# A per-sample matrix product with residual: the channel exchange in three copies for five, the slots of x at multiples of 2048 bytes, two slots a turn in VectorE's loop

## The chip, the cores and the metric

The kernel runs on one core of a Trainium2 chip. The core has five engines that run side by side and meet at semaphores: TensorE (PE, matrix products into PSUM), VectorE (DVE), ScalarE (ACT), GpSimd (POOL) and SyncE (SP, used here to issue transfers). 16 DMA engines move data between HBM (the chip's main memory) and the SBUF, the on-chip memory of 128 partitions. SP and ACT each have a queue of transfers. The metric is the device time of one execution in microseconds (us), the median of several.

## What is computed

```python
x: (128, 128, 1024) float32            # batch, channel, time
itok_B_0_7: (128,) int32, 0 to 7       # which matrix a sample uses
L0_cond_weights: (8, 128, 128) float32

w = weights[subjects]
out = jnp.einsum('bct,bcd->bdt', x, w)
return x + out
```

Each of the 128 samples is a 128 x 1024 block of x (512 KB). It is multiplied by one of eight matrices and added to itself. 67.1 MB are read for x and 67.1 MB written.

## The kernel before

**Slots.** The SBUF holds `x_all`, 12 slots of 4 samples (`H * G = 2 * 2`), 16 KB in each partition and 2 MB in all. 32 slots' worth of work (`NT = 32`, 4 samples each) run through the 12 slots in turn. x_all starts at a multiple of `ALIGN` = 4096 bytes: 16,512 bytes of each partition are taken ahead of it, a filler `room` of 3,968 bytes follows, and x_all begins at byte 20,480. Behind it lie the weights `w_all`, the unit matrix `eye`, `aside` (4 KB in all 128 partitions), and four 128 x 128 weight tiles `ws`.

**Loads.** ACT issues two loads of 1 MB for a slot (`load`, issued at line 72), one for each half h. A load reads two samples as one stretch of HBM and writes 8 KB into each partition. With that, a partition has two neighbouring channels of one sample (partitions 0 to 63 the half's first sample, 64 to 127 its second), where the product wants one channel of each sample.

**Exchange.** `trade` (line 157 for all its copies, in the helper `move`) mends that on ACT. Seen as halves h and places s, `both[A:, 0]` (partitions 64 to 127, place 0) and `both[:A, 1]` (partitions 0 to 63, place 1) change places, with A = 64. Five copies do so: two of 64x1024 put `both[A:, 0]` aside (one half into partitions 0 to 63 of `aside`, the other into 64 to 127), one of 64x2x1024 moves `both[:A, 1]` to `both[A:, 0]`, and two of 64x1024 bring what was put aside to `both[:A, 1]`. Each copy raises `s_moved`; ACT waits on it between the three steps and at the end. The last wait raises `s_half[0]`, on which PE's product waits.

**ACT's loop** takes four slots a turn (`AHEAD = 4`): wait for the slot's load, issue the loads of the slot four ahead (if that place is empty, `s_empty`), then exchange.

**PE** (`multiply`, line 208) computes for each half two samples, four matmuls into PSUM. The weight tile it uses is the matrix plus `eye` (so the product already holds the residual), with rows in the order of the exchanged channels; VectorE makes it (`place`, line 197).

**VectorE's loop** takes four slots a turn (`TURN = 4`). For each half of a slot: wait for the product (`s_product`), copy 128x2048 from PSUM over the slot (line 223), make the next slot's two weight tiles for this half. `s_product` counts within a turn and is lowered in the turn's last half (line 220).

**Stores.** SP waits for both halves of a slot (`s_added`) and issues its store of 2 MB; for the last 12 slots it stores two slots at once (4 MB). Slot 0's store is written differently (line 319) and is cut into 4 KB packets. In the last three stores two slots are read as one run of 32 KB in each partition, in the others each slot is a run of 16 KB. In HBM each sample's channel is a row of 4 KB. The order of the work is set by these queues and semaphores alone; there is no planner.

Of the kernel before, what the change touches and what calls it, by code (L numbers as in the profile page):

```python
# [30 lines left out]
G = 2  # L31
H = 2
# [18 lines left out]
R = 2  # L51

AHEAD = 4

MOVES = 5

TURN = 4

PLACED = 16

ALIGN = 4096
QUEUES = {mybir.EngineType.SP: "qSPDynamicHW", mybir.EngineType.Activation: "qActDynamicHW"}


# [21 lines left out]
def kernel(  # L86
# [7 lines left out]
    nc = tc.nc  # L94
    B, C, T = x.shape
    S, _, D = weights.shape
    NT = B // (G * H)

    def sbuf(name, *shape, dtype=F32):
        return ctx.enter_context(nc.sbuf_tensor(name, list(shape), dtype)).ap()  # L100


    room = -(nc.sbuf_base + -nc.sbuf_base % 32) % ALIGN
    if room:
        sbuf("room", C, room // 4)
# [4 lines left out]
    ]  # L110
    w_all = sbuf("w_all", C, S, D)
    w_raw, w_mid, w_late = (xs[SLOTS - 1][:, q, :] for q in range(3))
    A = C // R
    eye = sbuf("eye", C, 1, D)
    mark = sbuf("mark", 1, 1)
    aside = sbuf("aside", C, T)
    spare = [aside[h * A : (h + 1) * A] for h in range(H)]
    ws = [sbuf(f"w{i}", C, 1, D) for i in range(H * G)]
    zeros = xs[SLOTS - 1][:, H * G - 1, :N]
    given, near, wrap = (  # L120
        xs[SLOTS - 1][:1, H * G - 1, N + k * B : N + (k + 1) * B].bitcast(I32) for k in range(3)
# [18 lines left out]
    s_moved = tc.alloc_semaphore("s_moved")  # L140
# [15 lines left out]
    def move(out, in_):  # L156
        nc.scalar.copy(out, in_).then_inc(s_moved, 1)  # L157
# [4 lines left out]
    def trade(k, slot):  # L162
        base = slot * (H * G * T)
        both = x_all[:, bass.ds(base, H * G * T)].rearrange("c (h s t) -> c s h t", h=H, s=G)
        for h in range(H):
            move(spare[h], both[A:, 0, h])
        nc.scalar.wait_ge(s_moved, k * MOVES + H)
        move(both[A:, 0], both[:A, 1])
        nc.scalar.wait_ge(s_moved, k * MOVES + H + 1)
        for h in range(H):  # L170
            move(both[:A, 1, h], spare[h])
        nc.scalar.wait_ge(s_moved, (k + 1) * MOVES).then_inc(s_half[0], 1)

    def store(i, n):
# [10 lines left out]
    def subjects_of(i):  # L185
        _, subject = nc.values_load_multi_w_load_instructions(
            index[0:1, i] if isinstance(i, slice) else index[0:1, bass.ds(i * (H * G), H * G)],
            engines=[mybir.EngineType.DVE],
            min_val=0,
            max_val=S - 1,  # L190
            skip_runtime_bounds_check_because="the index is clamped on the chip above",
        )
        return subject

    def place(h, subject):
        for q in range(h * G, (h + 1) * G):
            copy = nc.vector.tensor_tensor(  # L197
                ws[q], w_all[:, bass.ds(subject[q], 1), :], eye, ALU.add
            )
        copy.then_inc(s_half[h], 1 if h else PLACED)  # L200
# [16 lines left out]
    def copy(slot, n, h):  # L217
        mine = x_all[:, bass.ds(slot * (H * G * T) + h * G * T, G * T)]
        n = n * H + h + 1
        product = nc.vector.wait_ge(s_product, n)  # L220
        if n == TURN * H:
            product.then_inc(s_product, -n)
        nc.vector.tensor_copy(mine, ps[h].rearrange("d g t -> d (g t)")).then_inc(s_added, 1)  # L223

    with tc.tile_critical():  # L225
# [31 lines left out]
        for r in range(R):  # L257
            if r:
# [6 lines left out]
                1.0,  # L265
                base=r - r * R * A,
                channel_multiplier=R,
# [7 lines left out]
        with nc.scalar.Fori(0, NT // AHEAD) as turn:  # L275
            for k in range(AHEAD):
                landed(k)
                with nc.scalar.If(turn < NT // AHEAD - 1):
                    empty = nc.scalar.wait_ge(s_empty, k + 1)
                    if k + 1 == AHEAD:  # L280
                        empty.then_inc(s_empty, -AHEAD)
                    load(
                        k,
                        (turn * AHEAD + (k + AHEAD)) % SLOTS,
                        nc.s_assert_within(
                            turn * (AHEAD * H * G) + (k + AHEAD) * H * G,
                            0,
                            B - H * G,
                            skip_runtime_bounds_check_because="the last turn loads nothing",
                        ),  # L290
                    )
                trade(k, (turn * AHEAD + k) % SLOTS)
            nc.scalar.wait_ge(s_moved, AHEAD * MOVES).then_inc(s_moved, -AHEAD * MOVES)

# [35 lines left out]
        for h in range(H):  # L330
            place(h, subject)
        with nc.vector.Fori(0, NT // TURN) as turn:  # L332
            for n in range(TURN):
                subject = subjects_of(turn * TURN + (n + 1))
                for h in range(H):
                    copy((turn * TURN + n) % SLOTS, n, h)
                    place(h, subject)
# [42 lines left out]
```

## Time and profile before

| What | Value |
|---|---|
| Three runs | 323.84 us median (323.23 to 324.43) |
| The profiled execution | 323.75 us |
| Its span, first to last instruction | 321.9 us |
| Granted clock of TensorE, mean | 0.921 |
| Bytes over the span | HBM read 67.63 MB, written 67.11 MB: 419 GB/s |
| VectorE: copies from PSUM, line 223 | 64 of 128x2048, 2.292 us each |
| TensorE: matmuls, line 208 | 512 of 128x512, 0.624 us each |

In a profile, a group of instructions is shown by line, engine, operation and operands (out<-in), with how many there were, their busy time, the mean duration in ns, and the idle time of the engine just before them with what ended it. "issue" means that the profile shows nothing that the engine waited for. The DMA row gives the busy share of the 16 DMA engines in 40 equal slices of the span, in tenths (9 is 90% or more). A packet is the piece of a transfer that one DMA engine moves at a stretch; a queue's row gives its packets, the MB and the share of the 16 engines' time that the packets took. In the table of stretches each row has the length, the busy time of PE, PE's weight loads, VectorE, ACT and POOL (with the count of instructions), the granted clock of TensorE, the DMA share and GB/s.

### The profile page before, as it was taken

To read this page: it belongs to the slowest core of one execution; us is meant where nothing else is said; L and a number is where in the kernel's file an instruction comes from. 1 tells how busy PE (TensorE), PEld (TensorE's weight loads), DVE (VectorE), ACT (ScalarE), POOL (GpSimd) and SP (SyncE) were. 2 spreads that over 40 slices of the span, in tenths; PEclk is the share of its full clock that TensorE was granted. 3 is DMA by queue.
4 is the path that set the end of the run, shared out by engine and by line. 5 is a ranking of instruction groups with operands and counts; after the bars stand their busy time and mean duration, and the time that the engine had idled before them with its cause. 6 is when DMAs were issued, how large, how long until landed. Compare 5 with 4: busy or idle time off the path is not lost. (4 is left out here: it accounts for less than half of the span.)

```text
span 321.9 us, 2680 instructions
## 1 busy us (share of the span) xinstructions
PE 247.3 (77%) x528; PEld 102.7 (32%) x528; DVE 181.4 (56%) x217; ACT 195.7 (61%) x162; POOL 2.5 (1%) x10
## 2 busy tenths in 40 slices
PE   7279988888888888759949799496784989999000
PEld 3034333333333333324314343242332434443000
DVE  4708765666666666663634847266552676787300
ACT  1577767776777776677275772747727689990000
POOL 0200000000000000000000000000000000000000
PEclk9969999999999999998978979799996999999755
DMA  8999999999999999999999999999999999999995
GB/s 326 391 456 444 405 390 430 438 430 432 417 421 432 425 428 428 432 452 407 425 423 425 423 423 419 421 428 438 446 423 405 432 450 403 428 446 432 419 432 220
DMA packets 7732, 134.76 MB, mean 419 GB/s; under 512 B 1457, under 2 KB 1458, under 8 KB 2098
## 3 DMA queue, kind: packets, MB, share of 16 engines
q1 hardware_dynamic: 4658, 67.64, 49.8%
q10 hardware_dynamic: 3072, 67.11, 49.0%
q14 instruction: 2, 0.02, 0.0%
HBM read 67.63 MB, written 67.11 MB: 419 GB/s over the span
## 5 line engine op out<-in xcount | busy, mean ns | idle before, releaser
L208 PE MATMUL ps<-x_all,w 128*128 x512 | 238.8, 624 | 49.0 <-PEq L204 48.8
L223 DVE COPY x_all<-ps 128x2048 f32 x64 | 146.7, 2292 | 113.7 <-PE ps L208 107.4
L208 PEld LDWEIGHTS ps<-x_all,w 128*128 128x128 f32 x512 | 99.1, 199 | 188.6 <-issue 188.3
L157 ACT COPY aside<-x_all 64x1024 f32 x64 | 66.7, 1042 | 82.4 <-issue 79.1
L157 ACT COPY x_all<-aside 64x1024 f32 x64 | 66.8, 1044 | 1.8
L157 ACT COPY x_all<-x_all x32 | 60.7, 1897 | 3.9
L197 DVE TENSOR_TENSOR w<-w_all,eye 128x128 f32<-128x128 f32 x132 | 31.8, 283 | 0.8 <-issue 0.8
L235 PE MATMUL ps<-x_all 128*128 128x512 f32 x16 | 8.6, 697 | 1.7 <-DVE x_all L232 1.7
L235 PEld LDWEIGHTS ps<-x_all 128*128 128x128 f32 x16 | 3.6, 230 | 5.8 <-issue 4.2
L273 ACT ACT_TABLE_LOAD x1 | 1.3, 1283 | 6.2 <-issue 6.2
L299 DVE COPY w_all<-x_all 32x256 f32<-32x256 f32 x12 | 3.9, 326 | 0.4
L244 DVE STREAM_TRANSPOSE x_all<-x_all 128x512 f32<-128x512 f32 x2 | 2.0, 1076 | 3.1 <-DMA x_all<-in_L_cond_weights_dram 3.1
L299 POOL COPY w_all<-x_all 32x256 f32<-32x256 f32 x4 | 1.7, 425 | 6.6 <-DVE x_all L296 6.4
L296 DVE STREAM_TRANSPOSE x_all<-x_all 128x1024 f32<-128x1024 f32 x1 | 1.2, 1226 | 0.0
L232 DVE MEMSET x_all<- 128x512 f32 x1 | 0.5, 485 | 1.0 <-SPq L225 1.0
L250 DVE TENSOR_SCALAR x_all<-x_all 1x128 int32<-1x128 int32 x1 | 0.2, 215 | 0.3 <-DMA x_all<-in_itok_B_dram 0.3
L260 POOL TENSOR_SCALAR_AFFINE_SELECT eye<-x_all 128x128 f32<-128x128 f32 x1 | 0.3, 292 | 1.4 <-DVE x_all L232 1.4
L254 DVE CUSTOM_DVE_ANT_0 index<-x_all 1x256 uint16<-1x256 uint16 x1 | 0.3, 278 | 0.0
L260 POOL TENSOR_SCALAR_AFFINE_SELECT eye<-eye 128x128 f32<-128x128 f32 x1 | 0.3, 292 | 0.1
L252 DVE TENSOR_SCALAR x_all<-x_all 1x128 int32<-1x128 int32 x1 | 0.2, 215 | 0.0
L273 ACT COPY mark<-eye 1x1 f32<-1x1 f32 x1 | 0.2, 190 | 0.0
L367 POOL MEMSET const-bfloat16-1.0<- 128x1 bf16 x1 | 0.1, 101 | 0.0
(5 smaller groups left out, 0.4 us busy)
## 6 DMA issues: line engine op xcount, KB each, us to landing
x_all<-in_x_dram ACTq DMA_DIRECT2D x64, 1024.0 KB, 11.7
out_dram<-x_all SPq DMA_DIRECT2D x20, 2048.0 KB, 54.1
out_dram<-x_all SPq DMA_DIRECT2D x6, 4096.0 KB, 31.4
x_all<-in_L_cond_weights_dram SPq DMA_DIRECT2D x1, 512.0 KB, 3.8
x_all<-in_itok_B_dram SPq DMA_DIRECT2D x1, 0.5 KB
```

What stands on the lines that cost most here:

```text
L157: nc.scalar.copy(out, in_).then_inc(s_moved, 1)
L197: copy = nc.vector.tensor_tensor(ws[q], w_all[:, bass.ds(subject[q], 1), :], eye, ALU.add)
L208: mm = nc.tensor.matmul(ps[h][:, q % G, t : t + N], ws[q][:, 0, :], x_all[:, bass.ds(at, N)], start=True, stop=True,)
L223: nc.vector.tensor_copy(mine, ps[h].rearrange("d g t -> d (g t)")).then_inc(s_added, 1)
L232: nc.vector.memset(zeros, 0.0).then_inc(s_zeros, 1)
L235: nc.tensor.matmul(ps[P_SLOTS - 1][:, G - 1, :N], zeros[:, :D], zeros, start=True, stop=True)
L244: nc.vector.transpose(w_mid.rearrange("p (e r h w j) -> p r j h e w", e=4, r=R, h=4, w=8)[:, r], w_raw.rearrange("p (j r d) -> p r j d", r ...
L254: nc.vector.tensor_tensor(index[:, :B], near, wrap, ALU.add).then_inc(s_index, 1)
L260: nc.gpsimd.affine_select(eye[:, 0], eye[:, 0] if r else zeros[:, :D], [[-1, D]], ALU.not_equal, 1.0, base=r - r * R * A, channel_multipli ...
L273: nc.scalar.copy(mark, eye[:1, 0, :1])
L296: nc.vector.transpose(w_late, w_mid).then_inc(s_sort, 1)
L299: engine.tensor_copy(w_all[32 * v : 32 * (v + 1), 2 * o : 2 * (o + 1), :], w_late[32 * o : 32 * (o + 1)].rearrange("c (e u r d) -> c u r e ...
```

## The change

Three things change.

- **Exchange.** `aside` becomes 64 partitions of 8 KB. One copy of 64x2048 puts both halves of `both[A:, 0]` aside, the middle copy stays, one copy of 64x2048 brings them back. `MOVES`, the count of `s_moved` for a slot, is 3 for 5.
- **Addresses.** `ALIGN` is 2048 for 4096. `eye`, two weight tiles and `mark` are allocated ahead of x_all, the filler shrinks to 352 bytes, and x_all begins at byte 18,432 of each partition, which is 9 x 2048, in place of 20,480, which is 5 x 4096.
- **VectorE's loop.** `TURN` is 2 for 4: 16 turns of two slots.

```diff
-MOVES = 5
+MOVES = 3

-TURN = 4
+TURN = 2

-ALIGN = 4096
+ALIGN = 2048

+    A = C // R
+    eye = sbuf("eye", C, 1, D)
+    ws = [sbuf(f"w{i}", C, 1, D) for i in range(G)]
+    mark = sbuf("mark", 1, 1)
     room = -(nc.sbuf_base + -nc.sbuf_base % 32) % ALIGN
     if room:
         sbuf("room", C, room // 4)
...
-    A = C // R
-    eye = sbuf("eye", C, 1, D)
-    mark = sbuf("mark", 1, 1)
-    aside = sbuf("aside", C, T)
-    spare = [aside[h * A : (h + 1) * A] for h in range(H)]
-    ws = [sbuf(f"w{i}", C, 1, D) for i in range(H * G)]
+    aside = sbuf("aside", A, H, T)
+    ws += [sbuf(f"w{i}", C, 1, D) for i in range(G, H * G)]
...
-        for h in range(H):
-            move(spare[h], both[A:, 0, h])
-        nc.scalar.wait_ge(s_moved, k * MOVES + H)
+        move(aside, both[A:, 0])
+        nc.scalar.wait_ge(s_moved, k * MOVES + 1)
         move(both[A:, 0], both[:A, 1])
-        nc.scalar.wait_ge(s_moved, k * MOVES + H + 1)
-        for h in range(H):
-            move(both[:A, 1, h], spare[h])
+        nc.scalar.wait_ge(s_moved, k * MOVES + 2)
+        move(both[:A, 1], aside)
         nc.scalar.wait_ge(s_moved, (k + 1) * MOVES).then_inc(s_half[0], 1)
```

The order of ACT's instructions in its loop, at the exchange of one slot (before with -, the change with +; "ISA" rows set up the copy's address):

```order
 L157 ISA
-L157 COPY aside<-x_all 64x1024
-L157 ISA
-L157 COPY aside<-x_all 64x1024
+L157 COPY aside<-x_all 64x2048
 L157 ISA
 L157 COPY x_all<-x_all 64x2x1024
-L157 COPY x_all<-aside 64x1024
-L157 ISA
-L157 COPY x_all<-aside 64x1024
+L157 COPY x_all<-aside 64x2x1024
```

Two copies stand where one stands now, on both sides of the middle one; the middle copy, the slot's two loads ahead of the exchange and everything else on ACT keep their places.

The order of VectorE's instructions at the end of a turn, in the changed kernel: the last half of the turn's second slot (line 221 is the copy from PSUM, line 195 makes a weight tile, line 330 is the loop).

```order
L221 ISA
L221 COPY x_all<-ps 128x2048
L195 ISA
L195 TENSOR_TENSOR w<-w_all,eye 128x128
L195 ISA
L195 TENSOR_TENSOR w<-w_all,eye 128x128
L330 REGISTER_ALU
L330 COMPARE_AND_BRANCH
```

Before, two more slots of the same instructions stood between the turn's second slot and these two rows of the loop; now the jump comes after every second slot.

## The prediction

> **What bounds the kernel now.** I read the profile's page first, its second part (busy tenths over the span) and its third (queues), because the busy shares of the engines are all under 80%.
>
> ```profile
> PE 247.3 (77%) x528; PEld 102.7 (32%) x528; DVE 181.4 (56%) x217; ACT 195.7 (61%) x162; POOL 2.5 (1%) x10
> ...
> DMA  8999999999999999999999999999999999999995
> ...
> DMA packets 7732, 134.76 MB, mean 419 GB/s; under 512 B 1457, under 2 KB 1458, under 8 KB 2098
> q1 hardware_dynamic: 4658, 67.64, 49.8%
> q10 hardware_dynamic: 3072, 67.11, 49.0%
> ```
>
> The reader is to see that the DMA row stands at 9 from the second slice to the last but one, and that the two queues (q10 is ACT's loads, q1 SP's stores and the weights) together fill 49.8 + 49.0 = 98.8% of the 16 DMA engines' time, 318.0 of 321.9 us. What is left is at the ends. The table by stretches says it more sharply:
>
> ```profile
> 0.00:2.00 2.00, 0.33 (x1) 0.33 (x2) 0.51 (x2) 0.00 (x0) 0.34 (x5) 1.00 0.03 2
> 2.00:318.00 316.00, 247.01 (x528) 102.35 (x527) 180.91 (x215) 195.71 (x162) 2.14 (x6) 0.93 1.01 426
> 318.00:322.00 4.00, 0.00 (x0) 0.00 (x0) 0.00 (x0) 0.00 (x0) 0.00 (x0) 0.50 0.06 25
> ```
>
> The last two numbers of a row are the DMA share and GB/s. For 316 us the share is full (1.01: packets are counted where they begin) at 426 GB/s; before it lie 2 us of start, behind it the completion of the last packets. So the time is 2 us, plus all packets at what each costs, plus the end. An edit counts if it changes what a packet costs, or opens a gap in that row.
>
> Next, whether work on the engines sets the end. The chain of waits breaks off at 301 us; the stores' tile and SP's own waits show what follows:
>
> ```profile
> L72 SPq DMA_DIRECT2D out_dram<-x_all x25: 560/1879/13552, 36.3 to 301.2; - x25
> DMA to landing us min/median/max: 19.7/51.4/59.2
> SPq L376 <- DMA out_dram<-x_all: 19.1, 1, 19.1
> 298.24 2.29 DVE L223 COPY x_all<-ps 128x2048 f32 x1 [0.79 <-DVEq L220]
> ```
>
> The last copy of VectorE ends at 300.5 us, the last store (4 MB) is issued at 301.2 and, by the shortest time to landing, has landed 19.7 us later. I get its own transfer from the price of its packets. Four stretches of the DMA view in which a queue moved packets of one size give all prices:
>
> ```profile
> q10 hardware_dynamic: 352, 7.86, 101.6%
> ```
> ```profile
> q1 hardware_dynamic: 354, 1.45, 25.3%
> ```
> ```profile
> q1 hardware_dynamic: 527, 8.11, 100.5%
> ```
> ```profile
> q1 hardware_dynamic: 200, 6.03, 100.9%
> ```
>
> The stretches are 10 to 28 us (loads of 32 KB: 7.86 MB is 240 of them, the rest are completions), 38 to 52 us (store 0, 354 packets of 4 KB), 268 to 287 us (stores of 16 KB, 495 of them) and 303 to 317 us (the last stores, 184 of 32 KB). Stretch times 16 times share over packets: a load packet costs 18 x 16 x 1.016 / 240 = 1.219 us, a 4 KB packet 14 x 16 x 0.253 / 354 = 0.160, a 16 KB store 19 x 16 x 1.005 / 495 = 0.617, a 32 KB store 14 x 16 x 1.009 / 184 = 1.228. The last store is 128 packets, 128 x 1.228 / 16 = 9.8 us. It waits 19.7 - 9.8 = 9.9 us behind older stores: **the engines could end 9.9 us later and the kernel would not**.
>
> ```profile
> x_all<-in_x_dram ACTq DMA_DIRECT2D x64, 1024.0 KB, 11.7
> out_dram<-x_all SPq DMA_DIRECT2D x20, 2048.0 KB, 54.1
> out_dram<-x_all SPq DMA_DIRECT2D x6, 4096.0 KB, 31.4
> ```
>
> The 64 loads are 64 x 32 = 2048 packets. 2098 - 1458 = 640 packets are of 4 KB (store 0 and the weights). Of the stores, 19 of 2 MB and three of 4 MB are (19 + 6) x 128 = 3200 packets of 16 KB, one for each partition and slot, and the last three, whose two slots are one run, 3 x 128 = 384 of 32 KB. Sum of all: 2048 x 1.219 + 640 x 0.160 + 3200 x 0.617 + 384 x 1.228, over 16 engines, is 156.0 + 6.4 + 123.4 + 29.5 = 315.3 us; the queues' 318.0 us hold 2.7 us of packets slower than their price.
>
> **The change part by part.** *Exchange.* The groups by line give the copies of ACT:
>
> ```profile
> L157 ACT COPY aside<-x_all 64x1024 f32 x64 | 66.7, 1042 | 82.4 <-issue 79.1
> L157 ACT COPY x_all<-aside 64x1024 f32 x64 | 66.8, 1044 | 1.8
> L157 ACT COPY x_all<-x_all x32 | 60.7, 1897 | 3.9
> 205.68 1.15 ACTq L72 DMA_DIRECT2D x_all<-in_x_dram  x2
> 207.01 2.11 ACT L157 COPY aside<-x_all 64x1024 f32 x2 [1.83 <-issue]
> 209.24 1.90 ACT L157 COPY x_all<-x_all  x1
> 211.17 2.11 ACT L157 COPY x_all<-aside 64x1024 f32 x2
> ```
>
> (The first three rows are of the page, the last four of the timeline.) Per slot two pairs of 64x1024 go, 2.11 us each with their overlap, and two copies of 64x2048 come. That shape is the middle row's, 1.897 us. So 4.22 us become 3.79, 0.42 us less per slot, 13.5 us of ACT over 32 slots, and the three waits per slot on s_moved stay three. On the path it is worth nothing: ACT already idles 79.1 us in front of its first copy, waiting for loads that stand in the full DMA queues. Its loads for the slot ahead are issued before the exchange, so at most those of the next slot are issued 0.42 us earlier, into the same queue. What is late next is the landing of that load, which is late now. At the end the 0.42 us disappear in the 9.9 us.
>
> *VectorE's loop.* Two slots a turn make 16 turns for 8, so the reset of s_product (line 220) and the jump run 8 times more.
>
> ```profile
> 112.53 2.29 DVE L223 COPY x_all<-ps 128x2048 f32 x1 [2.12 <-PE ps L208]
> 114.74 0.48 DVE L197 TENSOR_TENSOR w<-w_all,eye 128x128 f32<-128x128 f32 x2
> 116.01 2.29 DVE L223 COPY x_all<-ps 128x2048 f32 x1 [0.79 <-DVEq L220]
> ...
> 124.46 2.29 DVE L223 COPY x_all<-ps 128x2048 f32 x1 [0.68 <-PE ps L208]
> DVE x_all L223 <- DVEq L220: 6.3, 8, 0.8
> ```
>
> A second half that ends a turn starts 0.79 us after the weights before it (6.3 us in 8 times), one that does not 0.68 us: 0.1 us more, 0.9 us over 8 turns. It falls where VectorE next waits about 2 us for PE, as ahead of 112.53 and in most slots; without this cover it is 0.9 us, a tenth of the 9.9 us at the end. The last slot ends a turn before and after, so the last copy is not moved.
>
> *Addresses.* x begins at byte 18,432 of each partition in place of 20,480: every slot, every 8 KB that a load writes and every 4 KB row that a store reads now begins in the middle between two multiples of 4,096. This is the one edit that touches what the 98.8% are made of, and no packet of before has such an address. I bound it from both sides by the price of a cut. A load packet is one run in HBM and four of 8 KB in the SBUF (4 pieces); a 32 KB store is one run in the SBUF and eight rows in HBM (8 pieces). It costs 1.228 - 1.219 = 9 ns more for 4 more pieces, 2.3 ns a piece (the shares' last digit makes this 2.3 +- 0.4). If a 4 KB border of the SBUF costs as much as a cut, each of the 16,384 rows stored gets one in its middle, and each of the 8,192 runs loaded crosses two for one: 24,576 x 2.3 ns / 16 = 3.5 us. The low end is 0: the bytes and rows are the same, so no row of the trace has a gain to offer here. I take 0, because a load's 8 KB run already holds a border inside it, four in a packet; were these priced like cuts, a load would have 8 pieces and cost 1.228, not 1.219. The Trainium skill, DMA: Bandwidth & Descriptors, section "How a descriptor splits into AXI transactions", says that a descriptor starting at a multiple of 256 bytes is split into transactions of 256 bytes and that only a start off that grid adds one. Both bases are multiples of 256, so by that rule the sum gets 0, and 3.5 us only if 4 KB borders count as well, which no run here shows yet.
>
> *Order of tensors.* eye, two weight tiles and mark lie ahead of x, aside on 64 partitions; every instruction has its partners and waits as before. Cost 0; were an operand slower there, ACT, PE and DVE have the 9.9 us to hide it.
>
> **Sum.** The profiled execution took 323.75 us (span 321.9, and 1.85 around it), 0.09 below the median of the three runs, 323.84. To 323.75: exchange 0, loop 0, addresses 0 (to +3.5), order 0. **323.8 us.**
>
> **Rivals.** *Borders cost (slower).* Place: every packet, both queues. Price 3.5 us: 323.75 + 3.5 = 327.3. It shows as over 0.5% (1.6 us) from 1.6 x 16 / 24,576 = 1.05 ns a border. For it: nothing in the trace has such addresses, and no wait could hide it. Against it: the load packet's price. 0.13.
>
> *ACT's copies disturbed transfers (faster).* The 2.7 us of slow packets would go with fewer and shorter visits of ACT and other addresses: 323.75 - 2.7 = 321.1. Two stretches of the same stores, engines working and engines still:
>
> ```profile
> q1 hardware_dynamic: 174, 5.13, 100.2%
> ```
> ```profile
> 290.00:300.00 10.00, 7.99 (x19) 3.14 (x17) 7.67 (x10) 0.04 (x1) 0.00 (x0) 1.00 1.00 424
> 303.00:313.00 10.00, 0.00 (x0) 0.00 (x0) 0.00 (x0) 0.00 (x0) 0.00 (x0) 0.50 1.01 433
> ```
>
> From 290 to 302 us, with PE and VectorE at work until 300.9, 5.13 MB took 100.2% (157 packets, 12 x 16 x 1.002 / 157 = 1.225 us each); afterwards, with all engines still, 1.228. Engines do not lengthen a packet here, though ACT was still in both. The Trainium skill, SBUF — State Buffer, section "SBUF: two separate sides", says that DMA and engine accesses use different ports and cannot slow each other; the two prices agree, and by that rule this rival gives 323.75. 0.07.
>
> *The copies don't get shorter.* A slot has 2 x 2.10 MB / 426 GB/s = 9.85 us of transfers, ACT needs 213.28 - 205.68 = 7.6 us for it. With the pairs replaced it needs 7.2, so ACT would bind only if each 64x2048 copy to or from aside took (9.85 - 7.2) / 2 = 1.3 us more than 1.897; each 0.1 us above that for both costs 32 x 0.2 = 6.4 us. The middle copy has the same shape and both its sides in the SBUF. 0.03, slower; below that point it is the forecast.
>
> **How the numbers follow.** Within 0.5%, which is about what a measurement of this kernel can tell from no change (its three runs span 323.23 to 324.43): 0.77, the forecast, alone 322.6 to 325.0. Faster 0.07, from the second rival. Slower 0.13 + 0.03 = 0.16. The range reaches over the unknown price of a border to 327.3; below, 322.5 leaves the second rival out.
>
> **What would show it.** Right: the queues again at 98 to 99%, 426 GB/s from 2 to 318 us, ACT near 96 copies of 1.9 us and its idle time in front of the first one up by about 13 us, 16 waits on the reset in VectorE's loop. Wrong: in the same stretches a load packet above 1.219 us or a 16 KB store above 0.617 (1.228 and 0.626 are the border's full price); or a digit under 9 inside the DMA row.

## The result and the profile after

| Kernel | Median | Runs |
|---|---|---|
| before | 323.41 us | 22 |
| the change | 322.84 us | 22 |

The ratio is 0.998, with a 95% interval of 0.9971 to 0.9989. The change gains 0.6 us of 323. That is inside the 0.5% which the prediction called no change, but it is clear of zero, and the prediction had no term for it.

The page of the changed kernel, its busy shares, its DMA row and its queues:

```profile
PE 250.1 (78%) x528; PEld 103.4 (32%) x528; DVE 181.4 (56%) x217; ACT 183.6 (57%) x98; POOL 2.5 (1%) x10
...
DMA  8999999999999999999999999999999999999995
...
q1 hardware_dynamic: 4658, 67.64, 49.9%
q10 hardware_dynamic: 3072, 67.11, 49.0%
```

The DMA row is the same as before, digit for digit, and so are the counts of packets. ACT has 12.1 us less to do, and the span went from 321.9 to 321.2 us. The groups by line show the exchange:

```profile
L157 ACT COPY aside<-x_all 64x2048 f32 x32 | 60.7, 1897 | 95.0 <-issue 90.6
L157 ACT COPY x_all<-x_all x32 | 60.7, 1897 | 4.0
L157 ACT COPY x_all<-aside 64x2048 f32 x32 | 60.7, 1898 | 1.0
```

Each of the new copies takes what the middle copy took. ACT's idle time in front of the first copy rose from 82.4 to 95.0 us, by 12.6 us, about as much as it no longer works. In VectorE's loop the waits on the reset doubled in number and not in length:

```profile
DVE x_all L221 <- DVEq L218: 12.6, 16, 0.8
```

In this execution the engines ended later than before, and the kernel did not. VectorE's last copy and the last store:

```profile
300.76 2.29 DVE L221 COPY x_all<-ps 128x2048 f32 x1 [0.79 <-DVEq L218]
L72 SPq DMA_DIRECT2D out_dram<-x_all x25: 561/4571/12279, 36.2 to 303.7; - x25
DMA to landing us min/median/max: 16.5/53.8/58.7
```

The copy starts at 300.76 us for 298.24, the store is issued at 303.7 for 301.2, and it lands after 16.5 us for 19.7. So 2.5 us of the cover at the end were used and cost nothing. (In e4, the same program again, the last copy starts at 297.6 us, so the 2.5 us are of this execution and not of the change.)

The prices of packets in these stretches are those of before. The same stretches as in the prediction (10 to 28 us, 268 to 287 us, 303 to 317 us) of the DMA view of the changed kernel:

```profile
q10 hardware_dynamic: 351, 7.83, 101.2%
```
```profile
q1 hardware_dynamic: 526, 8.09, 100.3%
```
```profile
q1 hardware_dynamic: 198, 5.96, 99.8%
```

A load packet costs 18 x 16 x 1.012 / 239 = 1.219 us (1.219 before), a 16 KB store 19 x 16 x 1.003 / 494 = 0.617 (0.617), a 32 KB store 14 x 16 x 0.998 / 182 = 1.228 (1.228). In these stretches neither the border of 4,096 bytes nor anything else made a packet cheaper or dearer. The table by stretches shows where the 0.7 us between the two spans are (the last two numbers of a row are the DMA share and GB/s):

```profile
0.00:2.00 2.00, 0.33 (x1) 0.33 (x2) 0.50 (x2) 0.00 (x0) 0.34 (x5) 1.00 0.03 2
2.00:318.00 316.00, 249.79 (x528) 103.06 (x527) 180.86 (x215) 183.61 (x98) 2.14 (x6) 0.93 1.00 426
318.00:322.00 4.00, 0.00 (x0) 0.00 (x0) 0.00 (x0) 0.00 (x0) 0.00 (x0) 0.50 0.02 8
```

After 318 us the DMA engines still moved at 25 GB/s before and at 8 GB/s now: the same bytes were a little nearer to their end. Two sums over the packets' records say by what. All packets together took 318.1 us on each of 16 engines before and 317.6 after. The last engine finished 1.9 us after the mean of the 16 before, and 1.7 us after. So 0.5 us came from packets that took longer than their price, and 0.2 us from engines that finished more evenly. One execution of each can't say whether this is the change or the day; the experiments had to.

### The profile page after: what moved, and what is told of

The parts are those of the page before. It is cut to its first block, busy times and chain, and to the rows that moved or that the text cites. A ratio compares the mean times of both kernels' runs of the same rounds, so it can differ in the third digit from the quotient of the medians.

```text
span 321.2 us, 2576 instructions
## 1 busy us (share of the span) xinstructions
PE 250.1 (78%) x528; PEld 103.4 (32%) x528; DVE 181.4 (56%) x217; ACT 183.6 (57%) x98; POOL 2.5 (1%) x10
## 5 line engine op out<-in xcount | busy, mean ns | idle before, releaser
L157 ACT COPY aside<-x_all 64x2048 f32 x32 | 60.7, 1897 | 95.0 <-issue 90.6
L157 ACT COPY x_all<-aside 64x2048 f32 x32 | 60.7, 1898 | 1.0
L233 PE MATMUL ps<-x_all 128*128 128x512 f32 x16 | 10.2, 808 | 1.7 <-DVE x_all L230 1.7
```

The lines of the kernel that those rows point to most:

```text
L233: nc.tensor.matmul(ps[P_SLOTS - 1][:, G - 1, :N], zeros[:, :D], zeros, start=True, stop=True)
```

## The experiments

All ratios are against the kernel before on the same chip.

| Run | Kernel | Ratio | 95% interval |
|---|---|---|---|
| e1 | before again | 1.0000 | 0.9991 to 1.001 |
| e2 | addresses alone | 0.9999 | 0.999 to 1.0008 |
| e3 | addresses and exchange | 0.9978 | 0.9964 to 0.9991 |
| e4 | the change again | 0.9993 | 0.9984 to 1.0002 |
| e5 | before, loads eight slots ahead | 1.0622 | 1.0601 to 1.0644 |
| e6 | no exchange | 0.9979 | 0.997 to 0.9988 |
| e7 | six copies | 1.0245 | 1.022 to 1.027 |
| e8 | the change, loads eight slots ahead | 1.0621 | 1.0578 to 1.0664 |
| e9 | three copies early, five late | 0.9988 | 0.9979 to 0.9997 |
| e10 | five copies early, three late | 0.9978 | 0.9969 to 0.9987 |
| e11 | the change, ACT 2 us later | 0.9976 | 0.9966 to 0.9985 |
| e12 | before, x off the 256 byte grid | 1.0051 | 1.0032 to 1.0069 |

### Which part: e1 to e4

e1 is the kernel before, e4 the changed one, both unaltered. e2 and e3 differ from these by one line each:

```diff
 e2, from before
-ALIGN = 4096
+ALIGN = 2048
 e3, from the change
-TURN = 2
+TURN = 4
```

> The kernel before against itself, to see what two sets of runs of one program differ by. The change was measured at 0.998 of before (0.9971 to 0.9989), 0.6 us, in the two profiles as 0.5 us less of packets slower than their price (2.2 us before, 1.7 after by the same reckoning). If 0.6 us is chance between sets of runs, this kernel too may stand 0.1 to 0.2% off 1.000; if it is the change, this one stands at 1.000 within 0.1%.

> x at byte 18,432 with five copies and four slots a turn. If the addresses bring the 0.6 us: 0.998. If the exchange or the loop does, or chance: 1.000. If 4 KB borders cost anything and something else hides it: up to 1.011. Load packets 1.219 us and 16 KB stores 0.617 us in the same stretches as before by the forecast.

> x at byte 18,432 and three copies, four slots a turn: the change without VectorE's loop. Less e2 it is the exchange alone. If the exchange brings the 0.6 us: 0.998 here and 1.000 in e2. If the addresses do: 0.998 in both. If the loop does: 1.000 in both, and 0.998 only in e4.

> The change again. If the 0.6 us are of the change: 0.998 again (0.997 to 0.999). If they were chance between sets of runs: within 0.1% of 1.000.

A second set of runs of the same program stands at 1.0000, so two sets of one program can agree far better than 0.2% (e4 and the first measurement of the change, also one program, differ by 0.1%). The addresses alone do nothing. The stretches of e2's DMA view at 10 to 28 us, 268 to 287 us and 303 to 317 us:

```profile
q10 hardware_dynamic: 344, 7.60, 98.4%
```
```profile
q1 hardware_dynamic: 528, 8.13, 100.7%
```
```profile
q1 hardware_dynamic: 198, 5.96, 99.8%
```

are 18 x 16 x 0.984 / 232 = 1.222 us a load packet, 19 x 16 x 1.007 / 496 = 0.617 us a 16 KB store and 14 x 16 x 0.998 / 182 = 1.228 us a 32 KB store. The load packet is 3 ns above the 1.219 of before, but in the packets' records the median of this stretch is 1.213 us in both runs. The 3.5 us of the first rival are not there. By the rule of 256 bytes that the prediction set beside it (the Trainium skill, DMA: Bandwidth & Descriptors, section "How a descriptor splits into AXI transactions") there was nothing to expect of two bases that both are multiples of 256, and the run agrees within 0.1%.

With the exchange the gain appears: 0.9978 in e3, where VectorE's loop is still of four slots. e4 came out weaker, and its interval just holds 1.000; together with the first measurement (0.998) the change stands at about 0.999 to 0.998. The loop has no gain of its own to show: the kernels with it (0.998, 0.9993) are not faster than e3 without it. So the 0.6 us belong to the exchange, or to what comes with it in e3: e2 has the new base of x but still the old order of the other tensors, e3 has the new order too. Against the order speaks e6 below, which keeps the addresses of before and gains as much.

### How: loads further ahead, no exchange, a longer exchange (e5 to e8)

The trace of before gave a theory. The timeline of ACT in its first 45 us:

```profile
10.00 1.16 ACTq L72 DMA_DIRECT2D x_all<-in_x_dram  x2
11.33 2.11 ACT L157 COPY aside<-x_all 64x1024 f32 x2 [3.60 <-issue]
...
18.10 1.15 ACTq L72 DMA_DIRECT2D x_all<-in_x_dram  x2
19.42 2.11 ACT L157 COPY aside<-x_all 64x1024 f32 x2 [1.83 <-issue]
...
34.40 1.16 ACTq L72 DMA_DIRECT2D x_all<-in_x_dram  x2
...
43.01 1.27 ACTq L72 DMA_DIRECT2D x_all<-in_x_dram  x2
```

Loads are issued 8.1 to 8.2 us apart, once 8.6, and between one exchange and the next lie 1.83 us or little more, of which 1.15 are ACT's own issuing. After the first load it hardly waits for one here; its own length is the pace. In the packets' records the load packets in flight fall to two at 46.0 us and to none from 46.4 to 47.0, and 16 load packets take 1.53 to 2.05 us for 1.219. These start from 43.6 to 44.4 us, ahead of the gap in the loads; the expectations below take them for packets that start anew in it. Three copies bring each load forward. That is the theory of the dry queue. Its rival was that ACT's copies disturb transfers. In the edits, e7's later waits on `s_moved` are counted one up, and e6 leaves the exchange out, so its output is of unexchanged channels.

```diff
 e5 from before, e8 from the change
-AHEAD = 4
+AHEAD = 8
 e6, from before: the five copies of trade, replaced by one
+        move(token[:, k : k + 1], eye[:1, 0, :1])
 e7, from before: ahead of trade's copies (MOVES = 6)
+        move(spare[0], both[A:, 0, 0])
+        nc.scalar.wait_ge(s_moved, k * MOVES + 1)
```

> Five copies at byte 20,480, but loads eight slots ahead for four. The trace of before shows ACT issuing loads every 8.1 to 8.2 us up to 59 us, as long as its exchange and its issuing take, and the loads in flight falling from 12 to under 5 of 16 at 46 us; there some 16 load packets start anew together and take 0.4 to 0.9 us more each. Theory of the dry queue (three copies bring the next loads 0.42 us a slot earlier, so it dries less): this kernel, whose loads are further ahead, gains as much with five copies, 0.998. Theory that the copies of ACT disturb the transfers: 1.000, the copies are all there. Chance: 1.000.

> The exchange is left out (one 1x1 copy in its place), so the product and the output are of unexchanged channels; transfers are all there. Both the dry queue and the disturbance of transfers expect a gain of at least what three copies gave: 0.998 or less, down to 0.994 if all 1.9 us of slow packets go. If the exchange on ACT is off the path altogether, as the prediction had it: 1.000.

> One more copy of 64x1024 ahead of the five, so ACT needs about 9.3 us a slot for its exchange and its issuing, still under the 9.85 us of transfers. By the prediction (ACT binds only above 9.85 us): 1.000. By the dry queue: slower, a loss as large for 1.1 us more as three copies gained for 0.42 us less, or two to three times that, 1.002 to 1.005.

> The change with loads eight slots ahead. Dry queue: as e5 within 0.1%, 0.997 to 0.998, since in both the queue holds loads. Disturbance: as the change, 0.998 to 0.999, and below e5.

e5 and e8 told nothing of the theory, since another wait swallowed them. ACT's waits and its timeline in e5:

```profile
ACT aside L157 <- issue: 98.6, 24, 25.8
42.88 2.11 ACT L157 COPY x_all<-aside 64x1024 f32 x2
69.12 1.53 ACTq L72 DMA_DIRECT2D x_all<-in_x_dram  x2
```

With eight of 12 slots given to loads, the next load's place is empty only when a store of four slots before has landed. ACT waits for that ahead of its exchange, 25.8 us once, and the exchanges behind it stand still. It cost 20 us with either exchange. This is the price of a wait put in front of work that doesn't need it, and not an answer to the question.

e6 is an answer to a part. Its page:

```profile
PE 248.4 (77%) x528; PEld 103.5 (32%) x528; DVE 181.4 (57%) x217; ACT 7.6 (2%) x34; POOL 2.5 (1%) x10
...
DMA  8999999999999999999999999999999999999995
```

Taking away all 188 us of ACT's exchange gives 0.9979, no more than the 12 us that three copies take away. So the gain is not in proportion to ACT's copies, and what a shorter exchange can give this kernel ends at about 0.7 us (0.4 to 1.0 by the interval).

e7 is the largest effect of the study. One copy more, 1.08 us a slot, cost 7.1 us. Its DMA row, its first group of copies, ACT's waits (us in total, times, longest; e7's two rows, then the one of before), ACT's last copies (e7, then before) and e7's stores:

```profile
DMA  7999999999999999999999999999999999997747
...
L157 ACT COPY aside<-x_all 64x1024 f32 x96 | 100.1, 1042 | 63.4 <-issue 54.6
```
```profile
ACT aside L157 <- issue: 54.6, 26, 3.5
ACT aside L157 <- POOLq L315: 4.4, 2, 2.4
```
```profile
ACT aside L157 <- issue: 79.1, 28, 5.8
```
```profile
302.27 2.11 ACT L157 COPY x_all<-aside 64x1024 f32 x2
```
```profile
287.93 2.12 ACT L157 COPY x_all<-aside 64x1024 f32 x2
```
```profile
L72 SPq DMA_DIRECT2D out_dram<-x_all x25: 560/561/678, 37.7 to 315.1; - x25
DMA to landing us min/median/max: 11.5/27.7/38.1
```

Digits under 9 stand inside the DMA row, in its last four slices (in e5 and e8 they do too). The books can be kept to the end. 32 copies of 1.08 us (3.19 for 2.11 in the timeline) are 34.6 us of work. ACT's idle time "issue" before was 79.1 us in 28 times, of which 28 x 1.83 = 51.2 are its own issuing and 27.9 real waiting; in e7 it is 54.6 - 26 x 1.83 = 7.0, and 4.4 - 2 x 1.83 = 0.7 in the two waits put down to POOL. So 20.2 us were absorbed, and ACT's last copy should end 14.4 us later: it ends at 304.4 for 290.1, the last store is issued at 315.1 for 301.2. Its landing takes 11.5 us for 19.7, so 8.2 us more are absorbed by older stores that no longer stand ahead of it. 13.9 - 8.2 = 5.7 us are left, and the span is 327.6 for 321.9. (The profiled execution, 329.46 us, is the fastest of e7's five; their median is 7.1 us above that of before.)

### When: early or late in the run (e9 to e11)

In e9 and e10 the first two turns of ACT's loop (eight slots) are written out, with one kind of exchange, and the other six turns have the other kind. e11 holds ACT up once.

```diff
 e9 (e10 with 5, 3), from the change
-MOVES = 3
+FIRST, REST = 3, 5
 e11, from the change, ahead of ACT's loop
+        nc.scalar.wait_ge(s_in[0], DMA * H)
+        nc.scalar.copy(aside, xs[0].rearrange("c (h s) t -> c s h t", h=H)[A:, 0]).then_inc(s_moved, 1)
+        nc.scalar.wait_ge(s_moved, 1).then_inc(s_moved, -1)
```

> The change, with three copies for the first eight slots and five for the other 24 (the first two turns of ACT's loop written out). If the gain is made in the first 60 us, where ACT's own length sets when loads are issued (every 7.7 us for 8.2): 0.998, and no dry stretch at 43 to 46 us. If each exchange gives its share: a quarter of the gain, 0.9995.

> The mirror image of the same program: five copies for the first eight slots, three for the other 24. Gain made early: 1.000, and the dry stretch back at 43 to 46 us. Each exchange its share: three quarters of the gain, 0.9985.

> The change with one more copy of 64x2048 ahead of the first exchange, so all of ACT is about 2 us later once, and nothing else. Dry queue: the loads issued at 41.6 us in the change fall to 43.6, as before, so the gain goes, 1.000. If instead the shorter exchange counts slot by slot: 0.998 to 0.999, a single 1.9 us in a sum of 13 us.

e11 did to the loads what it was meant to do. Its timeline of ACT:

```profile
9.54 1.90 ACT L274 COPY aside<-x_all 64x2048 f32<-64x2048 f32 x1 [1.80 <-DMA x_all<-in_x_dram]
12.10 1.16 ACTq L72 DMA_DIRECT2D x_all<-in_x_dram  x2
...
43.65 1.42 ACTq L72 DMA_DIRECT2D x_all<-in_x_dram  x2
```

The loads of 41.72 us in the change went out at 43.65, later than the 43.01 of before, and the gain stayed whole: 0.9976. In its packets' records the queue of loads is as dry as before, with no load packet in flight from 45.8 to 47.6 us, and yet no load packet from 40 to 49 us takes over 1.4 us. So it isn't the late load that makes these packets slow, and the dry queue of the first 60 us is not where the gain comes from.

e9 and e10 do not tell early from late. The turns written out shortened ACT's pace by themselves: the loads of the first eight slots are issued 7.1 to 7.4 us apart in both, closer than in the change (7.7), so e10's five copies brought no dry stretch back. Both gain, e9 0.9988 and e10 0.9978, their intervals overlap, and both stand lower than the slot by slot theory expected (0.9995 and 0.9985).

### An address that does matter (e12)

```diff
 from before
-ALIGN = 4096
+ALIGN = 128
```

> Before with x at byte 16,512, which is 128 above a multiple of 256 (the 4,096 and 2,048 grids are both left). If a start off the 256 byte grid adds one transaction to each run of a packet, load packets (four runs) and 16 KB stores (one run) cost some ns more: at 4.7 ns a run, 128 bytes at 27 bytes a ns, 8,192 runs loaded and 3,584 stored make 3.5 us, 1.011. If any address does, as 18,432 did: 1.000.

x begins 128 bytes off the grid of 256, and the kernel is slower by 0.5%. Half of the 3.5 us worked out for one more piece a run is there, 1.65 us of the medians. The stretches of 10 to 28 us, 268 to 287 us and 303 to 317 us again:

```profile
q10 hardware_dynamic: 347, 7.70, 101.5%
```
```profile
q1 hardware_dynamic: 528, 8.13, 100.7%
```
```profile
q1 hardware_dynamic: 201, 6.06, 101.5%
```

give 0.617 us for a 16 KB store and 14 x 16 x 1.015 / 185 = 1.229 us for a 32 KB store, as on the grid. The load packet is dearer: 18 x 16 x 1.015 / 235 = 1.244 us for 1.219. These 25 ns for four runs are near the 4 x 4.7 = 19 ns of the expectation, but they are there only while the loads run alone: in the packets' records the median load packet of 100 to 260 us, among stores, takes 1.219 us in e12 and in before. So the dearer loads make 235 x 25 ns / 16 = 0.4 us in that stretch. The sum of all packets is 317.8 us, as in e1, and the last engine is 2.8 us behind the mean for 2.0 in e1. That is 0.8 us, as much as the span differs from before (322.7 for 321.9). Of the 1.65 us of the medians the rest isn't explained (the profiled execution is the fastest of e12's four), and why one engine is later wasn't tried.

## Why the prediction was right, and where it was off

**What bounds it** held. The DMA row, the 426 GB/s between 2 and 318 us and all prices of packets are the same, and no part of the change moved the time by more than 0.25%.

**Addresses, 0 (to +3.5):** 0 it is. e2 stands at 0.9999, and the row chosen to decide it, the load packet that already holds four borders inside, was the right one. One step of its working was rough: the shares of the stretches hold the completions too. In the packets' records of before a load packet from 10 to 28 us takes 1.215 us in the mean and a 32 KB store 1.228, so a piece is 3.3 ns for 2.3, and the upper bound 5.1 us for 3.5. The run shows nothing of either.

**VectorE's loop, 0:** nothing measurable. There are 16 waits of 0.8 us for 8, under waits for PE, as said.

**Exchange, "on the path it is worth nothing":** this term is off by 0.6 us. The copies took 1.897 us and ACT idled 12.6 us longer, as worked out, and still e3, e6, e10, e11 and the first measurement agree on about 0.2%. What the runs show: the gain comes with the exchange, it is no larger when all copies go, and it is not made by an earlier issue of loads (in e11 the loads up to 52 us go out later than in before, from 12.10 for 10.00 us to 51.59 for 51.24). In the profiled executions of the five-copy kernels (before, e1, e2) the packets' sum is 318.1, 317.8 and 317.8 us and the last engine 1.9 to 2.2 us behind the mean; in the three-copy ones (after, e3, e4) 317.6, 317.2 and 317.2, and 1.4 to 1.7. So it looks as if the gain lay half in packets slower than their price and half in how evenly the engines finish. These are single executions, and the five-copy ones happen to be 0.3 to 0.6 us above their kernels' medians; in e11, with three copies, the last engine is 1.9 us behind.

One place holds as much as the whole difference of the sums: the 16 load packets that start from 43.2 to 44.4 us and take 1.53 to 2.11 us in before, e1 and e2. Together they are 0.5 to 0.7 us above their price on each of the 16 engines. In after, e3 and e4 no load packet from 40 to 49 us takes over 1.4 us. What makes them slow stays open: e11 has the dry queue and e12 five copies, and neither has these packets. With that, the way by which a shorter exchange gains 0.6 us stays open as well: the dry queue fell with e11, disturbance in proportion to the copies with e6.

The step's reason was wrong in one thing. It read "79.1 us idle" as waiting for loads. Of that, 51.2 us are ACT's own issuing of loads, 1.83 us before each exchange, and in the first 60 us it hardly waits for loads at all.

**The third rival's point of decision, "ACT would bind only" above 9.85 us a slot,** was wrong, and e7 showed it: ACT bound with 7.6 + 1.1 us by the prediction's count, 9.2 with everything between (ACT's exchanges ran from 11.2 to 304.4 us, 293.2 / 32; the count leaves out 0.5 us a slot between the last copy and the next issue, 17.6 to 18.10 in the timeline of before). The mistake was to compare rates and to forget that the last slot's work is followed by product, copies and a 4 MB store which no longer overlap with any load. The 9.9 us of cover were sized too large as well. They took the last store's landing alone to be its 9.8 us of transfer, and it is 11.5 us in e7 and in e5, where no older store stands ahead of it, so the cover is 19.7 - 11.5 = 8.2 us. The last exchange may then end 8.2 us later than in before, at 298.3 us, and (298.3 - 11.3) / 32 = 9.0 us a slot is, by this estimate, where ACT binds. The forecast wasn't touched, because the change goes the other way.

**The second rival, ACT's copies disturb transfers,** gave 321.1 us. With no copies at all the time is 322.6 for 323.3, so of its 2.7 us some 0.7 exist, and 1.0 at most by the interval.

## What to carry to other kernels

Where the DMA row is full from end to end, price the packets first: here edits that left their count, size and price alone moved the time by tenths of a per cent, even when they took all 188 us of copies off an engine. An engine that is not the bound has a cover, and the cover is a sum over the run and not a rate: count its real waiting (without its own issuing of transfers) and the work in the queue behind its last step. Here 12 us less on ACT gave 0.6 us, and 35 us more took 7.

## What was not expected of the hardware

- Two loads issued by ACT keep it for 1.83 us (1.15 us of issuing in the timeline and the steps around it), which the profile counts as idle time "issue". Over 28 slots that is 51 us on an engine whose copies take 194.
- A base of x that is 4,096 or 2,048 bytes aligned makes no difference (0.9999); 128 bytes off the grid of 256 costs 0.5%. A load packet is 25 ns dearer there while loads run alone (10 to 28 us), and among stores its median is unchanged (1.219 us).
- In all profiled executions that end with the transfers (the DMA row full to its last slice but one), one of the 16 engines finishes 1.0 to 2.8 us after the mean of them, and the end of the kernel waits for that one.
